# Masking local-attention scores with VectorE adds instead of TensorE matmuls, in half of the tile steps of a macaron block

## The chip, the cores and the metric

The kernel runs on one core of a Trainium2 chip. The metric is the device time of one execution in microseconds (us); three executions of the kernel before are given, and one further execution was recorded by the hardware profiler. A core has five instruction streams that matter here: TensorE (PE in the profile, with its weight loads shown apart as PEld), VectorE (DVE), ScalarE (ACT), GpSimd (POOL), and SyncE (SP), which issues all DMAs here.

## The reference

The input is x with 2048 tokens of 128 features. The block is half of a feed-forward transformer stack, a state space layer, and half of the same stack again:

```python
x = x + 0.5 * ffn_ref(layernorm(x), ...)     # 6 layers
x = x + attn_ref(layernorm(x), ...)          # state space layer (Mamba), one layer
x = x + 0.5 * ffn_ref(layernorm(x), ...)     # the same 6 layers again
```

Each of the 6 layers shifts half of the features by one token, makes queries, keys and values for 16 heads of 64, scales queries and keys to unit norm, rotates them, attends in windows of 32 tokens to the window itself and the one before, projects, adds the residual, and then does a gated feed-forward with a layer norm. What the change touches is the mask of the scores:

```python
mask = (it < jb) | (it > jb + w) | (jb == -1)
sim = jnp.einsum('bhwie,bhwje->bhwij', bq, bk2) * QK_SCALE
sim = jnp.where(mask, -jnp.finfo(sim.dtype).max, sim)
attn = jax.nn.softmax(sim, -1)
```

All arithmetic of the kernel is fp32, except that the mask is multiplied in bf16 in the kernel before.

## The kernel before

**Tiles.** The tokens are cut in tiles of 128 (four windows of 32). One pass of the stack over half of the tokens (a segment of 8 tiles) through 6 layers is 48 tiles. There are 192 tiles g = 0 to 191: first stack, segment 0 (0 to 47) and segment 1 (48 to 95), then second stack, segment 0 (96 to 143) and segment 1 (144 to 191). The state space layer of the 8 blocks of 256 tokens runs beside tiles of the middle two quarters: block s starts at step 48 + 12 s and takes some 18 steps, so it lasts from step 48 to about step 150. In the first quarter and the last one the tiles have no such work beside them.

**Steps.** The program is written out as a software pipeline. At step i each stage of the table ORDER is issued for tile g = i - lag, in the order of the table's third column (its place within the step); the stages of the state space layer are merged into the same order by their own times. [...]Feed-forward stages work on two tiles at once, so a stage of them is issued in every second step only, and steps come in two kinds:

- In every step TensorE does, in this order: the averages PX (L596), the projection of queries PQ (L372), a transpose XT (L568), the scores S (L500 masks, L511 products), the projection of keys PK (L372), the mixing ZM (L617), the transposes of queries and keys RQ and RK (L453).
- An even step adds Y (L744) ahead of PX, and F1 (L656) between S and PK. An odd step adds V (L678) ahead of PX, G (L698) between PK and ZM, and A (L698) after ZM.
- VectorE does, in every step: UK (L414, sum of squares of the keys before), SM (L546, L547, divisors), T2Q and T1Q (L398, L391, the rotation's products on the queries), MX (L528, the maxima), UQ (L414), TP (L561, the transpose of the probabilities), T1K and T2K (L391, L398, the same products on the keys), RS (L633, the residual). An odd step adds VT (L317, L318) after SM and H (L730) after RS; an even step adds YR (L758) after UK.
- ScalarE does, among others, SQ (L384, squares), ES (L522, the copy of the scores to SBUF), SK (L384), EX (L541, exponents). GpSimd does CQ and CK (L440), SB (L535, scores less maxima), AQ and AK (L408), DV (L551).

**Score stages.** S is issued at lag 2. For each parity of the heads, one bf16 matmul of a 32-row selection matrix with a 32 x 64 mask (repeated over 8 heads) starts the accumulation in a bank, and 64 small matmuls add the products. In a first tile of the sequence (`st.tok` 0) a second mask is added, which hides the window before the first. Then VectorE takes the maxima from the banks and ScalarE copies the scores to the SBUF tile `pr`. GpSimd subtracts the maxima in SBUF.

**Banks.** [...]Six form three pairs `w0`, `w1`, `w2`; `bank2` gives the pair that has been free longest, and `used` counts a pair's readers. The seventh bank is the tag "n", single: XT, F1, ZM, V and Y write into it in turn, and each must wait until the reader of the one before is done (ZM is read by RS, V by VE and VT, XT by ScalarE's L575). The last is the tag "y".

```python
    def bank(self, name, tag="n"):
        return self.ps.tile([P, 512], F32, tag=tag, name=name)
```

The tile `sq` of squares is single too (SQ, SK write it, UQ, UK read it).

Of the kernel before, what the change touches and what calls it, by code (L numbers as in the profile page):

```python
# [9 lines left out]
F32 = mybir.dt.float32  # L10
BF16 = mybir.dt.bfloat16
AF = mybir.ActivationFunctionType
ALU = mybir.AluOpType
AX = mybir.AxisListType
# [3 lines left out]
P = 128  # L18
# [3 lines left out]
HEADS = 16  # L22
DH = 64
INNER = HEADS * DH
WIN = 32
# [5 lines left out]
MASKED = -1.0e25  # L31
# [18 lines left out]
C_MASK = 256  # L50
C_MASK0 = C_MASK + 2 * WIN
C_PICK = C_MASK0 + 2 * WIN
C_PICK0 = C_PICK + P
C_RATIO = C_PICK0 + P
C_ALL = C_RATIO + 1
EXP_LN = 6
ST = 8
# [63 lines left out]
class Stream:  # L121
# [11 lines left out]
    def __init__(self, k, x, out, wp, sb, rp, ps):  # L133
        self.k, self.nc, self.x, self.out = k, k.nc, x, out
        self.wp, self.sb, self.ps = wp, sb, ps
        self.at, self.w, self.sub = [], [Ctx() for _ in range(2 * UNITS)], {}
        for g in range(TILES):
            st = Ctx()
            st.again, r = divmod(g, UNITS * ST)
            st.seg, r = divmod(r, DEPTH * ST)  # L140
            st.layer, st.t = divmod(r, ST)
            st.w = self.w[g // ST]
            st.tok = st.seg * SEG + st.t * P
            st.x, st.rot, st.sq, st.t2 = {}, {}, {}, {}
            self.at.append(st)
        self.ff = [Ctx() for _ in range(TILES // 2)]
        self.tabs = {}
        self.r0 = [rp.tile([P, SEG + 1], F32, tag=f"r0{i}", name="r0") for i in range(2)]
        self.r1 = rp.tile([P, SEG + 1], F32, tag="r1", name="r1")

        self.c0 = rp.tile([P, DEPTH], F32, tag="c0", name="c0")
        self.c1 = rp.tile([P, DEPTH], F32, tag="c1", name="c1")
        self.b1 = rp.tile([P, DEPTH, 2, 3], F32, tag="b1", name="b1")
        self.todo = {}
        self.pairs, self.pair_of, self.returned = [[0, i - 3] for i in range(3)], {}, 0
# [336 lines left out]
    def score(self, g):  # L492

        nc, k, st = self.nc, self.k, self.at[g]
        st.s = self.bank2(("s_ps", g), 2).rearrange("p j (c k) -> p j c k", k=2 * WIN)
        for par in range(2):
            rows = slice(64 * par, 64 * par + 32)
            masks = [k.mask] if st.tok else [k.mask, k.mask0]
            for lhs, rhs in masks:
                nc.tensor.matmul(  # L500
                    out=st.s[:, par],
                    lhsT=lhs[rows],
                    rhs=rhs[rows].unsqueeze(1).to_broadcast([32, 8, 2 * WIN]),
                    start=lhs is k.mask[0],
                    stop=False,
                )
        for c in range(8):
            for b in range(4):
                for par in range(2):
                    rows = slice(64 * par, 64 * par + 64)  # L510
                    nc.tensor.matmul(  # L511
                        out=st.s[32 * b : 32 * b + 32, par, c, :],
                        lhsT=st.qt[rows, c, bass.ts(b, WIN)],
                        rhs=st.kt[rows, c, bass.ds(WIN * b, 2 * WIN)],
                        start=False,
                        stop=(c == 7),
                    )

    def scores_out(self, g):
        st = self.at[g]  # L520
        st.pr = self.sb.tile([P, HEADS, 2 * WIN], F32, tag="pr", name="pr")
        self.nc.scalar.copy(st.pr.rearrange("p (c j) k -> p j c k", j=2), st.s)  # L522
        self.used("s_ps", g)

    def maxima(self, g):
        st = self.at[g]
        st.mx = self.sb.tile([P, HEADS], F32, tag="mx", name="mx")
        self.nc.vector.tensor_reduce(  # L528
            st.mx.rearrange("p (c j) -> p j c", j=2), st.s, AX.X, ALU.max
        )  # L530
        self.used("s_ps", g)

    def less(self, g):
        st = self.at[g]
# [664 lines left out]
@with_exitstack  # L1199
def macaron_kernel(  # L1200
    ctx: ExitStack,
    tc: tile.TileContext,
    x: bass.AP,
    in_w: bass.AP,
    xp_w: bass.AP,
    dt_w: bass.AP,
    out_w: bass.AP,
    wqk: bass.AP,
    wv: bass.AP,
    wo: bass.AP,  # L1210
    w1: bass.AP,
    w2: bass.AP,
    scales: bass.AP,
    vecs: bass.AP,
    cst: bass.AP,
    tabs: bass.AP,
    out: bass.AP,
):
    nc = tc.nc
    k = Ctx()  # L1220
    k.nc, k.tc = nc, tc
    k.d_in_w, k.d_xp_w, k.d_dt_w, k.d_out_w = in_w, xp_w, dt_w, out_w
    k.d_wqk, k.d_wv, k.d_wo, k.d_w1, k.d_w2, k.tabs = wqk, wv, wo, w1, w2, tabs
    k.d_sc = scales

    const = ctx.enter_context(tc.tile_pool(name="const", bufs=1))
    cs = const.tile([P, C_ALL], F32, tag="cs", name="cs")
    nc.sync.dma_start(out=cs, in_=cst)
    k.ident = cs[:, C_ID : C_ID + P]
    k.cen = cs[:, C_CEN : C_CEN + P]  # L1230
    masks = const.tile([P, 2, 2 * WIN + P], BF16, tag="masks", name="masks")
    nc.vector.tensor_copy(
        masks[:, :, 0 : 2 * WIN],
        cs[:, C_MASK : C_MASK + 4 * WIN].rearrange("p (a k) -> p a k", a=2),
    )
    nc.vector.tensor_copy(
        masks[:, :, 2 * WIN :], cs[:, C_PICK : C_PICK + 2 * P].rearrange("p (a k) -> p a k", a=2)
    )
    k.mask, k.mask0 = ((masks[:, j, 2 * WIN :], masks[:, j, 0 : 2 * WIN]) for j in range(2))
    k.ratio = cs[:, C_RATIO : C_RATIO + 1]  # L1240
    k.pv = const.tile([P, V_ALL], F32, tag="pv", name="pv")
    nc.sync.dma_start(out=k.pv, in_=vecs)
    k.ones = const.tile([P, P], F32, tag="ones", name="ones")
    nc.vector.memset(k.ones, 1.0)
    k.minus_g = const.tile([P, DEPTH], F32, tag="minus_g", name="minus_g")
    nc.vector.tensor_scalar(k.minus_g, k.pv[:, V_G : V_G + DEPTH], -1.0, None, ALU.mult)
    k.minus_nw = const.tile([P, 1], F32, tag="minus_nw", name="minus_nw")
    nc.vector.tensor_scalar(k.minus_nw, k.pv[:, V_NW : V_NW + 1], -1.0, None, ALU.mult)
    k.eps = const.tile([P, 1], F32, tag="eps", name="eps")
    nc.vector.memset(k.eps, LN_EPS)  # L1250
    k.minus_one = const.tile([P, 1], F32, tag="minus_one", name="minus_one")
    nc.vector.memset(k.minus_one, -1.0)
    k.zero = const.tile([P, 1], F32, tag="zero", name="zero")
    nc.vector.memset(k.zero, 0.0)
    xt = const.tile([P, N], F32, tag="xt", name="xt")

    dram = ctx.enter_context(tc.tile_pool(name="dram", bufs=1, space=bass.MemoryType.DRAM))

    def kept(name, shape, count):
        return [dram.tile(shape, F32, tag=f"{name}{i}", name=f"{name}{i}") for i in range(count)]  # L1260

    k.merged = kept("m", [P, 2 * INNER], DEPTH)
    k.scaled_w1 = kept("w1s", [P, 2 * FF], DEPTH)
    k.scaled_tabs = [kept(f"tab{i}_", [P, 8 * DH], 8) for i in range(DEPTH)]
    k.last_keys = kept("lk", [P, 8 * WIN], DEPTH)
    k.last_inputs = kept("li", [WIN, P], DEPTH)
    k.bc = kept("bc", [2 * NS, SUB], 8)

    with (
        tc.tile_pool(name="weights", bufs=2) as wp,  # L1270
        tc.tile_pool(name="residuals", bufs=1) as rp,
        tc.tile_pool(name="tiles", bufs=2) as sb,
        tc.tile_pool(name="banks", bufs=1, space=PSUM) as ps,
        ExitStack() as pools,
    ):
        t = Stream(k, xt, out, wp, sb, rp, ps)
        with tc.manual_schedule(engines=MANUAL):
            t.run(x, pools)


def shape_constants():


    cst = np.zeros((P, C_ALL), np.float32)
# [5 lines left out]
    cst[:, C_MASK : C_MASK + 2 * WIN] = np.where((s >= q) & (s <= q + WIN), 0.0, MASKED)  # L1290
    cst[:, C_PICK : C_PICK + P] = q == np.arange(P)[None, :] % WIN
    cst[:, C_MASK0 : C_MASK0 + 2 * WIN] = np.where((q == 0) & (s < WIN), MASKED, 0.0)
    cst[:, C_PICK0 : C_PICK0 + P] = (q == 0) & (np.arange(P)[None, :] < WIN)

    half = np.arange(0, DH, 2, dtype=np.float32)
# [12 lines left out]
    tabs = kinds.reshape(4, NB, 4, P, DH).transpose(3, 1, 0, 2, 4)  # L1308
    cst[:, C_RATIO] = np.tile(base ** (P // (WIN // 2)), 2)
    return cst, np.ascontiguousarray(tabs.astype(np.float32))  # L1310


def laid_out(i):
# [23 lines left out]
    qs, ks = i["L0_ffn_q_scale"], i["L0_ffn_k_scale"]  # L1337
    scales = np.stack([qs, swapped(qs), ks, swapped(ks)], 1).reshape(DEPTH, 4 * DH)
    cst, tabs = shape_constants()
    w = i["L0_ffn_Wqkv"]  # L1340
    return {
# [36 lines left out]
```

## Time and profile before

| | |
|---|---|
| time, median of 3 runs | 3321.47 us (3318.79 to 3322.2) |
| the profiled execution: own time, span | 3318.65 us, 3316.7 us |
| granted TensorE clock, mean | 0.996 |
| busy: PE, DVE, ACT, POOL | 97%, 85%, 77%, 88% |
| DMA queues, share of 16 engines | 18.0%, 0.7%, 0.5% |
| mask matmuls L500 | 408, 384 ns each, 77.5 us busy together |
| maxima L528 on DVE | 192, 1214 ns each |
| copies of scores L522 on ACT | 192, 1019 ns each |

The profile gives busy times of each engine, the waits that it infers from semaphores, and the chain of work that ended last. A busy time is the union of the instructions' spans; the ends of matmuls are modelled and overlap the starts of the next ones. The trace's timeline gives start, duration, engine, line, what is written and read, and the idle time just ahead with what ended it.

### The profile page before, as it was taken

The numbers are of one execution on the slowest core, as the hardware profiler recorded it, in microseconds if no ns is written. First come the engines' busy times: TensorE is split into PE (matmuls) and PEld (weight loads), VectorE is DVE, ScalarE is ACT, GpSimd is POOL, SyncE is SP. The second block draws the span as 40 slices with busy tenths as digits, with TensorE's granted clock in tenths as the row PEclk, the third lists the DMA queues.
The fourth block names the chain that finished last, engine by engine and source line by source line (L and its number), as shares of the span: only waits on it lengthen the run. The fifth ranks groups of instructions, "written<-read, shape, count | busy, mean of one in ns | idle before, by whom it ended". The sixth has DMA issues, their size and how long they took to land.

```text
span 3316.7 us, 97481 instructions
## 1 busy us (share of the span) xinstructions
PE 3207.2 (97%) x41936; PEld 2225.6 (67%) x41936; DVE 2802.8 (85%) x3540; ACT 2551.6 (77%) x4121; POOL 2907.3 (88%) x2317
## 2 busy tenths in 40 slices
PE   7999999999999999999999999999999999999997
PEld 4677677676666666666666666666666676777765
DVE  5778888887898989889989889898988888888884
ACT  6777777778778778787787877877777777777775
POOL 6999999998988989889888898898988888988983
PEclk9999999999999999999999999999999999999999
DMA  8222221221211122121211122111121111111000
GB/s 259 76 67 65 66 67 58 71 68 45 59 52 43 47 53 56 50 61 37 56 51 54 47 53 57 42 52 53 52 63 39 31 41 44 32 36 43 20 11 9
DMA packets 134494, 181.26 MB, mean 55 GB/s; under 512 B 13176, under 2 KB 91312, under 8 KB 127152
## 3 DMA queue, kind: packets, MB, share of 16 engines
q1 hardware_dynamic: 134064, 175.04, 18.0%
q8 instruction: 330, 5.41, 0.7%
q14 instruction: 100, 0.82, 0.1%
HBM read 138.75 MB, written 24.05 MB: 49 GB/s over the span
## 4 chain that ended last, share of the span: by engine, by line
PE 69%; DVE 12%; ACT 9%; POOL 7%; issue 2%; DMA 0%; SPq 0%; POOLq 0%; DVEq 0%; ACTq 0%
PE x_ps L372 16%; PE y_ps L617 16%; PE z_ps L596 8%; PE t_ps L453 8%; PE s_ps L511 6%; PE g_ps L698 3%; PE o_ps L744 3%; PE a_ps L698 3%; DVE da L1055 2%; DVE rot L391 2%; POOL rot L440 2%; DVE t L398 2%; PE y_ps L1089 2%; ACT da L1044 1%; ACT sq L384 1%
## 5 line engine op out<-in xcount | busy, mean ns | idle before, releaser
L408 POOL TENSOR_TENSOR rot<-rot,t 128x1024 f32<-128x1024 f32 x384 | 900.7, 2368 | 10.6 <-DVE rot L391 6.1
L372 PE MATMUL x_ps<-qk,r 128*128 128x512 f32 x1536 | 753.4, 613 | 29.6 <-ACT zt L608 10.1
L617 PEld LDWEIGHTS y_ps<-zt,m 128*128 128x128 f32 x6144 | 715.1, 192 | 63.8 <-ACT xc L667 36.6
L440 POOL TENSOR_TENSOR rot<-rot,rn 128x1024 f32<-128x1024 f32 x384 | 722.4, 1902 | 14.4
L617 PE MATMUL y_ps<-zt,m 128*128 128x128 f32 x6144 | 718.6, 275 | 5.3 <-ACT xc L667 3.1
L384 ACT ACTIVATE sq<-x_ps 128x1024 f32<-128x1024 f32 x384 | 393.2, 1024 | 276.3 <-DVE rot L391 229.9
L398 DVE TENSOR_TENSOR t<-x_ps,tab 128x1024 f32<-128x1024 f32 x384 | 467.7, 1218 | 154.6 <-PE i_ps L568 84.4
L551 POOL TENSOR_TENSOR pr<-pr,rs 128x1024 f32<-128x1024 f32 x192 | 365.2, 1902 | 198.8 <-DVE rs L547 174.0
L372 PEld LDWEIGHTS x_ps<-qk,r 128*128 128x128 f32 x1536 | 271.7, 190 | 361.8 <-issue 232.8
L391 DVE TENSOR_TENSOR rot<-x_ps,tab 128x1024 f32<-128x1024 f32 x384 | 467.3, 1217 | 20.0 <-ACT sq L384 19.5
L608 ACT COPY zt<-z_ps 128x1024 f32<-128x1024 f32 x384 | 368.9, 1010 | 140.8 <-PE z_ps L596 140.6
L414 DVE TENSOR_REDUCE ss<-sq 128x16 f32<-128x1024 f32 x384 | 466.5, 1215 | 7.7 <-ACT sq L384 5.0
L596 PE MATMUL z_ps<-pt,xw 32*128 32x512 f32 x3072 | 402.5, 614 | 3.1 <-DVE t L398 1.4
L535 POOL TENSOR_TENSOR pr<-pr,mx 128x1024 f32<-128x1024 f32 x192 | 365.3, 1903 | 25.9 <-ACT carry L1066 19.4
L453 PE MATMUL t_ps<-cs,rot 128*128 128x128 f32 x3072 | 370.9, 273 | 4.3 <-DVE sc L1076 2.1
L453 PEld LDWEIGHTS t_ps<-cs,rot 128*128 128x128 f32 x3072 | 344.1, 141 | 32.7 <-issue 9.8
L511 PE MATMUL s_ps<-kt,qt 64*32 64x64 f32 x24576 | 287.3, 225 | 0.5 <-issue 0.5
L511 PEld LDWEIGHTS s_ps<-kt,qt 64*32 64x32 f32 x24576 | 255.9, 105 | 47.1 <-issue 46.0
L541 ACT ACTIVATE pr<-pr 128x1024 f32<-128x1024 f32 x192 | 203.2, 1058 | 106.9 <-POOL pr L535 106.1
L596 PEld LDWEIGHTS z_ps<-pt,xw 32*128 32x128 f32 x3072 | 146.6, 184 | 163.4 <-issue 129.6
L561 DVE STREAM_TRANSPOSE pt<-pr 128x1024 f32<-128x1024 f32 x192 | 237.0, 1234 | 2.3 <-POOL pr L551 2.3
L546 DVE TENSOR_REDUCE rs<-pr 128x16 f32<-128x1024 f32 x192 | 232.9, 1213 | 6.2 <-ACT pr L541 3.3
(144 smaller groups left out, 4809.0 us busy)
## 6 DMA issues: line engine op xcount, KB each, us to landing
bc<-bc SPq DMA_DIRECT2D x64, 512.0 KB, 5.4
tab<-tab SPq DMA_DIRECT2D x120, 256.0 KB, 2.6
qk<-in_wqk_dram SPq DMA_DIRECT2D x24, 1024.0 KB, 5.0
m<-m SPq DMA_DIRECT2D x24, 1024.0 KB, 5.3
tab<-in_tabs_dram SPq DMA_DIRECT2D x48, 256.0 KB, 2.9
xw<-xw SPq DMA_DIRECT2D x192, 48.0 KB, 3.3
m<-mst SPq DMA_DIRECT2D x6, 1024.0 KB
w<-w1s SPq DMA_DIRECT2D x18, 341.0 KB, 3.5
```

Of the source, the lines that this page charges most:

```text
L372: nc.tensor.matmul(out=x[:, j], lhsT=self.columns(g), rhs=st.w.qk[:, bass.ds(kind * INNER + j * 512, 512)], start=True, stop=True,)
L384: self.nc.scalar.activation(st.sq[kind], st.x[kind], AF.Square)
L391: self.nc.vector.tensor_tensor(st.rot[kind], st.x[kind], cos, ALU.mult)
L398: self.nc.vector.tensor_tensor(st.t2[kind].rearrange("p h (two c) -> p h two c", two=2), st.x[kind].rearrange("p h (two c) -> p h two c", ...
L408: self.nc.gpsimd.tensor_tensor(st.rot[kind], st.rot[kind], st.t2[kind], ALU.add)
L414: self.nc.vector.tensor_reduce(st.ss[:, kind, :], st.sq[kind], AX.X, ALU.add)
L440: self.nc.gpsimd.tensor_tensor(st.rot[kind], st.rot[kind], st.rn[:, kind, :].unsqueeze(2).to_broadcast([P, HEADS, DH]), ALU.mult,)
L453: self.nc.tensor.transpose(t_ps[:, c, :], flat[:, bass.ts(c, P)], self.k.ident)
L511: nc.tensor.matmul(out=st.s[32 * b : 32 * b + 32, par, c, :], lhsT=st.qt[rows, c, bass.ts(b, WIN)], rhs=st.kt[rows, c, bass.ds(WIN * b, 2 ...
L596: self.nc.tensor.matmul(out=st.z[b // 2][:, b % 2].rearrange("p (h q) -> p h q", q=WIN), lhsT=st.xw[rows, j, :], rhs=st.pt[rows, :, j, :], ...
L608: self.nc.scalar.copy(st.zt[:, 2 * half : 2 * half + 2].rearrange("p b h q -> p b (h q)"), st.z[half])
L617: self.nc.tensor.matmul(out=st.y_ps.rearrange("p (b q) -> p b q", q=WIN), lhsT=st.w.m[:, h // 2, h % 2, :], rhs=st.zt[:, :, h, :], start=( ...
```

## The change

A tile is `quiet` when its stack number equals its segment number: tiles 0 to 47 and 144 to 191, 96 of 192. For a quiet tile

- S issues no mask matmuls; each product matmul starts and stops its own 32 x 64 output;
- ES does nothing: no ScalarE copy;
- MX makes the tile `pr`, adds the mask to the scores in two VectorE instructions (one for each bank, 128 x 512, PSUM and a repeated 128 x 64 fp32 mask in SBUF, to SBUF), and takes the maxima from `pr` in SBUF. Both counts of the pair are given back there.

The constants get 64 more columns for the mask of a first tile (C_FIRST), 32 KB more in the load of `cst` at the start. For other tiles the code is as before. ORDER, and with it the place of MX, is the same.

```diff
+            st.quiet = st.again == st.seg
...
     def score(self, g):
...
-        for par in range(2):
-            rows = slice(64 * par, 64 * par + 32)
-            masks = [k.mask] if st.tok else [k.mask, k.mask0]
-            for lhs, rhs in masks:
-                nc.tensor.matmul(
...
+        if not st.quiet:
+            for par in range(2):
...
-                        start=False,
-                        stop=(c == 7),
+                        start=st.quiet,
+                        stop=st.quiet or c == 7,
                     )
 
     def scores_out(self, g):
         st = self.at[g]
+        if st.quiet:
+            return
...
     def maxima(self, g):
-        st = self.at[g]
+
+        nc, k, st = self.nc, self.k, self.at[g]
         st.mx = self.sb.tile([P, HEADS], F32, tag="mx", name="mx")
-        self.nc.vector.tensor_reduce(
-            st.mx.rearrange("p (c j) -> p j c", j=2), st.s, AX.X, ALU.max
-        )
-        self.used("s_ps", g)
+        if st.quiet:
+            st.pr = self.sb.tile([P, HEADS, 2 * WIN], F32, tag="pr", name="pr")
+            mask = k.added if st.tok else k.added0
+            mask = mask.unsqueeze(1).to_broadcast([P, 8, 2 * WIN])
+            pr = st.pr.rearrange("p (c j) k -> p j c k", j=2)
+            for par in range(2):
+                nc.vector.tensor_tensor(pr[:, par], st.s[:, par], mask, ALU.add)
+            self.used("s_ps", g)
+            self.used("s_ps", g)
+            nc.vector.tensor_reduce(st.mx, st.pr, AX.X, ALU.max)
+        else:
+            nc.vector.tensor_reduce(
+                st.mx.rearrange("p (c j) -> p j c", j=2), st.s, AX.X, ALU.max
+            )
+            self.used("s_ps", g)
```

More of the change, by code (lines that the diff above doesn't have):

```diff
@@ L53 @@
 C_PICK0 = C_PICK + P
-C_RATIO = C_PICK0 + P
+C_FIRST = C_PICK0 + P
+C_RATIO = C_FIRST + 2 * WIN
 C_ALL = C_RATIO + 1
@@ L495, in score @@
         st.s = self.bank2(("s_ps", g), 2).rearrange("p j (c k) -> p j c k", k=2 * WIN)
-        for par in range(2):
-            rows = slice(64 * par, 64 * par + 32)
-            masks = [k.mask] if st.tok else [k.mask, k.mask0]
-            for lhs, rhs in masks:
[L500 to L505, printed above, removed]
-                )
+        if not st.quiet:
+            for par in range(2):
+                rows = slice(64 * par, 64 * par + 32)
+                masks = [k.mask] if st.tok else [k.mask, k.mask0]
+                for lhs, rhs in masks:
+                    nc.tensor.matmul(
+                        out=st.s[:, par],
+                        lhsT=lhs[rows],
+                        rhs=rhs[rows].unsqueeze(1).to_broadcast([32, 8, 2 * WIN]),
+                        start=lhs is k.mask[0],
+                        stop=False,
+                    )
         for c in range(8):
@@ L525, in maxima @@
     def maxima(self, g):
-        st = self.at[g]
+        nc, k, st = self.nc, self.k, self.at[g]
         st.mx = self.sb.tile([P, HEADS], F32, tag="mx", name="mx")
-        self.nc.vector.tensor_reduce(
-            st.mx.rearrange("p (c j) -> p j c", j=2), st.s, AX.X, ALU.max
-        )
-        self.used("s_ps", g)
+        if st.quiet:
[11 more added lines that the diff above has]
+                st.mx.rearrange("p (c j) -> p j c", j=2), st.s, AX.X, ALU.max
+            )
+            self.used("s_ps", g)
     def less(self, g):
@@ L1239, in macaron_kernel @@
     k.mask, k.mask0 = ((masks[:, j, 2 * WIN :], masks[:, j, 0 : 2 * WIN]) for j in range(2))
+    k.added = cs[:, C_MASK : C_MASK + 2 * WIN]
+    k.added0 = cs[:, C_FIRST : C_FIRST + 2 * WIN]
     k.ratio = cs[:, C_RATIO : C_RATIO + 1]
@@ L1292, in shape_constants @@
     cst[:, C_MASK0 : C_MASK0 + 2 * WIN] = np.where((q == 0) & (s < WIN), MASKED, 0.0)
+    cst[:, C_FIRST : C_FIRST + 2 * WIN] = cst[:, C_MASK : C_MASK + 2 * WIN]
+    cst[0:WIN, C_FIRST : C_FIRST + WIN] = MASKED
     cst[:, C_PICK0 : C_PICK0 + P] = (q == 0) & (np.arange(P)[None, :] < WIN)
```

## The prediction

> **What bounds the kernel now.** I read the busy shares first, then a window for each quiet stretch (the tiles without state space work beside them), then the chain of waits there, then the timeline of one pair of steps, since an even and an odd step together repeat.
>
> ```profile
> PE 3207.2 (97%) x41936; PEld 2225.6 (67%) x41936; DVE 2802.8 (85%) x3540; ACT 2551.6 (77%) x4121; POOL 2907.3 (88%) x2317
> PE 69%; DVE 12%; ACT 9%; POOL 7%; issue 2%; DMA 0%; SPq 0%; POOLq 0%; DVEq 0%; ACTq 0%
> 120.00:780.00 660.00, 652.79 (x9018) 461.82 (x9019) 541.02 (x677) 504.11 (x781) 617.22 (x486) 1.00 0.20 66
> 2610.00:3230.00 620.00, 620.00 (x8604) 441.02 (x8606) 519.07 (x635) 475.30 (x728) 544.33 (x423) 1.00 0.11 33
> ```
>
> The last two lines are the quiet stretches; after the length come busy PE, PEld, DVE, ACT, POOL. PE has no gap (652.79 of 660, 620.00 of 620), DVE is at 82% and 84%. The chain in the second stretch is PE alone, piece after piece:
>
> ```profile
> 2912.07 0.32 PE s_ps L500 x2
> 2912.39 1.41 PE s_ps L511 x91
> ...
> 2919.72 1.75 PE t_ps L453 x16
> 2921.47 0.43 PE v_ps L678 x2
> 2921.90 1.93 PE z_ps L596 x16
> ```
>
> So each pair of mask matmuls is 0.32 us of the engine that sets the pace. But a saturated engine also says that the others arrive just in time or earlier; how much earlier is what the change spends. VectorE in the same even step (start, duration, line; idle time ahead in brackets):
>
> ```profile
> 2912.05 1.23 DVE L398 TENSOR_TENSOR t<-x_ps,tab 128x1024 f32<-128x1024 f32 x1 [1.38 <-PE x_ps L372]
> 2913.19 1.21 DVE L391 TENSOR_TENSOR rot<-x_ps,tab 128x1024 f32<-128x1024 f32 x1
> 2914.33 1.21 DVE L528 TENSOR_REDUCE mx<-s_ps 128x16 f32<-128x1024 f32 x1
> ...
> 2919.01 1.21 DVE L398 TENSOR_TENSOR t<-x_ps,tab 128x1024 f32<-128x1024 f32 x1
> 2920.14 0.58 DVE L633 TENSOR_TENSOR r<-y_ps,r 64x128 f32<-64x128 f32 x2
> 2921.20 0.30 PEld L678 LDWEIGHTS v_ps<-sq,ones 128*128 128x128 f32 x2
> ```
>
> It is released by the end of PQ, and from T2Q at 2912.05 to the end of RS at 2920.72 (2920.14 + 0.58) it has no idle time at all. RS reads the mixing result out of the single bank "n". V, the next writer of that bank on PE, loads at 2921.20, only 0.48 after. That V waits for RS is seen where RS came late, at the start of the kernel:
>
> ```profile
> 119.33 0.57 DVE L633 TENSOR_TENSOR r<-y_ps,r 64x128 f32<-64x128 f32 x2
> 120.02 0.30 PEld L678 LDWEIGHTS v_ps<-sq,ones 128*128 128x128 f32 x2 [0.40 <-issue]
> 120.05 0.67 PE L678 MATMUL v_ps<-sq,ones 128*128 128x256 f32 x2 [0.19 <-DVE r L633]
> ```
>
> Here the load follows RS's end (119.90) by 0.12, PE having been idle. So V's slack is 0.48 - 0.12 = 0.36 us.
>
> [...]1217 ns for 1024 from PSUM (L391), 424 ns for 256 (L993), which gives 688 for 512 on a straight line.[...]ACT's squares of the queries start at 2914.44, after T1Q's end at 2914.40 on the same banks.
>
> **The change, part by part**, for a quiet tile.
>
> *Removed from PE*: two mask matmuls, 0.32 us on the chain (four for a first tile, one tile in each of 6 layers). At most 96 x 0.32 + 6 x 0.32 = 33 us.
>
> *Removed from ACT*: one copy L522, 1.02 us. ACT is 77% busy, and the squares around it wait for VectorE, so I give nothing for it. The subtraction on POOL loses this source and waits for the maxima alone.
>
> *Added on DVE*: two adds of 128x512. A following instruction starts about 0.08 before the end of the one ahead (L391 at 2917.86 lasts 1.23, L398 starts at 2919.01), so the first add takes 0.69 - 0.08 = 0.61; the second feeds the maxima and is taken whole, 0.69, with 0.03 ahead of a dependent instruction (L546 ends at 2923.10, L547 starts at 2923.13). The maxima keep their 1.21: L414 reads SBUF at 1215 ns, L528 PSUM at 1214. Sum 1.33 us. The operation in this form is not in the trace: below it is bounded by 2 x 0.61 = 1.22, above by 2 x 0.69 + 0.06 = 1.44. No reason for a gain here.
>
> *Behind it on DVE, even step*: UQ, TP, T1K, T2K, RS, then UK, SM. None of them waited before, so RS is 1.33 later, against a slack of 0.36: V comes 0.97 later. [...]PX, PQ, XT behind V are 0.97 later as well, though their own data is there. The 0.32 saved earlier in this step is lost in front of V. Nothing is later next: T2K's banks, which PX takes over, are free before RS; XT needs VT, and RS to VT (UK, SM, L547, VT: 3.5 us) is shorter than V to XT (4.4).
>
> *Odd step*: T2Q starts when PQ ends, as before. PE would be 0.32 ahead after S, but G takes over the queries' pair, which ScalarE squares only after T1Q:
>
> ```profile
> 2928.24 1.02 ACT L384 ACTIVATE sq<-x_ps 128x1024 f32<-128x1024 f32 x1 [1.40 <-DVE rot L391]
> 2929.38 1.12 PEld L698 LDWEIGHTS g_ps<-q,w 128*128 128x128 f32 x6 [0.70 <-issue]
> ```
>
> G loads 0.12 after the squares' end at 2929.26, so it cannot come forward by more than about 0.1. Then T2K is 1.33 later; RQ loads 1.40 after T2K's end at 2934.03 and takes over its pair, a slack of 1.40 - 0.12 = 1.28: about 0.05 late. After T2K, VectorE has waits of 0.53 (RS), 0.79 (H), 0.58 (YR) and 1.38 (T2Q), 3.28 in all, which take up the rest. Odd steps: nothing, between -0.1 and +0.2.
>
> *POOL and the queues*: L535 starts at 2917.49 behind CK, the maxima end at 2915.54 + 1.33: still covered by 0.6. No DMA moves[...].
>
> *Sum*. The gap from RS to V repeats over a layer's four even steps: 0.46, 0.46, 0.78, 0.24 in the first stretch, 0.47, 0.47, 0.47, 0.18 in the second (means 0.48 and 0.40; slacks 0.36 and 0.28). Even steps with V behind them: 22 in the first, some 22 in the second that are not covered by the last state space block. 22 x (1.33 - 0.36) + 22 x (1.33 - 0.28) = 21 + 23 = 44 us. The first steps, before there is a V, and the tail may give back 2. So +42: the profiled execution's own 3318.65 would be 3361; the median of the runs lies 2.8 above it, so **3363 us**.
>
> **Rivals.** *Faster*: V is not held, the mask matmuls' time is gained. This would need RS's place on DVE not to depend on MX, or an add that overlaps other work. For it speaks the saturated PE and DVE at only 84%; against it the unbroken DVE row above. Price: -33 us would be 3289; but with G held by the squares (and ZM in even steps by XC, loading at 2915.78 right after XC behind those squares) about 0.25 a pair of steps, 47 pairs, -12: 3310. It wins only if the delay at RS is under 0.36, so an addition of under a third of 1.33. Chance 0.12. *No change*: the delay is about 0.5, or the two effects cancel; 3321, chance 0.04. *My forecast*: chance 0.68, with additions of 1.22 to 1.44 (44 even steps x 0.11 = 5 us either way) and odd steps of -0.1 to +0.2 (-4 to +9): 3350 to 3378. *Slower still*: VectorE also stops the odd steps at RQ, or POOL's second addition L408, which in even steps starts at 2921.7 while T2K would end at 2921.55, becomes late: 0.3 to 0.5 a pair more, +14 to +23, 3377 to 3386. Chance 0.16. That the adds are not issued as said has no sign in the diff.
>
> **The numbers.** About 0.2% (6.6 us) is what can be told from no change here. Slower 0.68 + 0.16 = 0.84, faster 0.12, same 0.04. The slower cases' own range is 3338 to 3390; to hold 8 in 10 the range begins at 3325 and ends at 3392.
>
> **What would show it.** Right: in quiet even steps DVE runs unbroken from T2Q to RS, 1.33 us longer; ahead of V a repeating PE gap of about 1.3 us named after L633; the pair of steps takes about 31.7 instead of 30.74; middle stretch as before; DVE's two adds at about 0.69 each. Wrong: pairs of 30.5 or less, no gap at V; or adds of under 0.5 us.

## The result and the profile after

The changed kernel takes 3367.25 us (median of 4 runs, 3366.33 to 3370.48) against 3320.18 us before in the same runs: a ratio of 1.0143, interval 1.0125 to 1.0161. It is slower by 47 us. The profiled execution took 3370.48 us (span 3368.3). In the changed file the residual RS is L650, the variances V are L695, T2Q and T2K L400, T1Q and T1K L393, the adds L540.

The page's busy shares, the engines' shares of the chain, and two windows of the quiet stretches (length; busy PE, PEld, DVE, ACT, POOL; clock):

```profile
PE 3207.9 (95%) x41732; PEld 2216.4 (66%) x41732; DVE 2917.3 (87%) x3732; ACT 2465.4 (73%) x4025; POOL 2913.6 (86%) x2317
PE 53%; DVE 26%; ACT 10%; POOL 7%; issue 3%; DMA 0%; SPq 0%; DVEq 0%; POOLq 0%; ACTq 0%
120.00:780.00 660.00, 633.94 (x8706) 444.71 (x8705) 573.86 (x740) 451.77 (x716) 604.47 (x475) 0.99 0.20 63
2640.00:3280.00 640.00, 617.38 (x8519) 435.33 (x8521) 567.07 (x716) 439.80 (x691) 545.67 (x422) 1.00 0.10 32
```

PE was busy for all of 620 us in the second stretch before; now 22.6 of 640 us are idle, though PE has less to do. VectorE's share of the chain has more than doubled, yet at 567 of 640 us VectorE is not full. The waits by engine name the place:

```profile
PE v_ps L695 <- DVE r L650: 34.4, 42, 1.1
PE g_ps L715 <- ACT sq L386: 13.1, 42, 0.8
```

Each line gives the sum, the number of waits and the longest one. Before, the first pair stood with 0.7 us in 2 waits and the second, the wait of G in odd steps, with 3.6 us in 5. The timeline of one even step and the start of the next one, VectorE first, then PE's loads and matmuls:

```profile
2982.52 1.23 DVE L400 TENSOR_TENSOR t<-x_ps,tab 128x1024 f32<-128x1024 f32 x1 [1.38 <-PE x_ps L374]
2983.67 1.22 DVE L393 TENSOR_TENSOR rot<-x_ps,tab 128x1024 f32<-128x1024 f32 x1
2984.80 1.28 DVE L540 TENSOR_TENSOR pr<-s_ps,cs 128x512 f32<-128x512 f32 x2
2986.11 1.22 DVE L543 TENSOR_REDUCE mx<-pr 128x16 f32<-128x1024 f32 x1
...
2990.75 1.22 DVE L400 TENSOR_TENSOR t<-x_ps,tab 128x1024 f32<-128x1024 f32 x1
2991.99 0.15 DVE L646 COPY r<-c 64x1 f32<-64x1 f32 x1
2992.16 0.59 DVE L650 TENSOR_TENSOR r<-y_ps,r 64x128 f32<-64x128 f32 x2
```

```profile
2989.82 1.78 PEld L455 LDWEIGHTS t_ps<-cs,rot 128*128 128x128 f32 x16
2992.87 0.30 PEld L695 LDWEIGHTS v_ps<-sq,ones 128*128 128x128 f32 x2 [1.27 <-ACT qt L464]
2992.90 0.67 PE L695 MATMUL v_ps<-sq,ones 128*128 128x256 f32 x2 [1.06 <-DVE r L650]
```

The maxima start 1.31 us after the first add does (2984.80 to 2986.11), so that is what the adds put in front of everything behind them. VectorE then runs without a gap to RS, which ends at 2992.75 (2992.16 + 0.59), and V's load follows 0.12 later, after 1.27 us of idle weight loading. (This is one of the every-fourth even steps that has the small copy L646 in front of RS.) The load row names ACT, the matmul row DVE: of two releasers named for one wait, the one that had just ended is RS (L464 ended at 2992.01). What stands behind V in PE's program came later with it: the averages PX had their probabilities (L578 ended at 2989.60) and their banks (T2K ended at 2991.97), but their first matmul is at 2993.50, 0.60 after V's, where it was 0.53 after V's before (2921.30 to 2921.83).

How much later RS is shows in an ordinary even step of the changed kernel, from T2Q to the end of RS:

```profile
2760.47 1.22 DVE L400 TENSOR_TENSOR t<-x_ps,tab 128x1024 f32<-128x1024 f32 x1 [1.60 <-PE x_ps L374]
2769.82 0.58 DVE L650 TENSOR_TENSOR r<-y_ps,r 64x128 f32<-64x128 f32 x2
```

That is 9.93 us (2769.82 + 0.58 - 2760.47), against 8.67 before (2912.05 to 2920.72). So of the 1.31 us, 1.26 arrive at RS. Part of the rest is a short wait that the timeline doesn't mark: before, UQ started 1.17 after the maxima (2914.33 to 2915.50), and now it starts 1.14 after them (2986.11 to 2987.25).

From XT of an even step to XT of the next, the timeline gives 13.78 us before (2911.80 to 2925.58), and now 14.70, or 14.98 in steps like this one. The odd step takes 16.96 in both.

### The profile page after: what moved, and what is told of

Read it like the earlier page. It is cut to its first block, busy times and chain, and to the rows that moved or that the text cites. A ratio compares the mean times of both kernels' runs of the same rounds, so it can differ in the third digit from the quotient of the medians.

```text
span 3368.3 us, 97252 instructions
## 1 busy us (share of the span) xinstructions
PE 3207.9 (95%) x41732; PEld 2216.4 (66%) x41732; DVE 2917.3 (87%) x3732; ACT 2465.4 (73%) x4025; POOL 2913.6 (86%) x2317
## 4 chain that ended last, share of the span: by engine, by line
PE 53%; DVE 26%; ACT 10%; POOL 7%; issue 3%; DMA 0%; SPq 0%; DVEq 0%; POOLq 0%; ACTq 0%
PE x_ps L374 12%; PE y_ps L634 11%; PE z_ps L613 8%; DVE rot L393 6%; DVE t L400 6%; PE t_ps L455 5%; PE g_ps L715 3%; PE o_ps L761 3%; PE a_ps L715 3%; DVE ss L416 3%; PE s_ps L514 2%; ACT sq L386 2%; DVE da L1072 2%; POOL rot L442 2%; DVE pt L578 2%
## 5 line engine op out<-in xcount | busy, mean ns | idle before, releaser
L410 POOL TENSOR_TENSOR rot<-rot,t 128x1024 f32<-128x1024 f32 x384 | 901.7, 2370 | 12.3 <-DVE rot L393 6.4
L400 DVE TENSOR_TENSOR t<-x_ps,tab 128x1024 f32<-128x1024 f32 x384 | 467.9, 1219 | 187.8 <-PE i_ps L585 113.1
L393 DVE TENSOR_TENSOR rot<-x_ps,tab 128x1024 f32<-128x1024 f32 x384 | 467.6, 1218 | 13.4 <-ACT sq L386 12.8
L578 DVE STREAM_TRANSPOSE pt<-pr 128x1024 f32<-128x1024 f32 x192 | 237.2, 1235 | 2.1 <-POOL pr L568 2.1
```

The costliest lines, as they stand in the source:

```text
L393: self.nc.vector.tensor_tensor(st.rot[kind], st.x[kind], cos, ALU.mult)
L400: self.nc.vector.tensor_tensor(st.t2[kind].rearrange("p h (two c) -> p h two c", two=2), st.x[kind].rearrange("p h (two c) -> p h two c", ...
L410: self.nc.gpsimd.tensor_tensor(st.rot[kind], st.rot[kind], st.t2[kind], ALU.add)
```

## The experiments

The theory: V waits for RS because the bank "n" is single, RS stands behind the adds in VectorE's order, and PX, PQ and XT stand behind V in PE's. Its rival: work added to VectorE counts wherever it stands. All times are medians, ratios are against the kernel before in the same runs.

**odd_tiles and even_tiles.** The change for one parity of the quiet tiles.

```diff
-            st.quiet = st.again == st.seg
+            st.quiet = st.again == st.seg and g % 2 == 1
```

> The adds only for quiet tiles with an odd number, so MX with adds falls in odd steps (lag 2), where V is not behind RS; even quiet tiles as before. Theory (V in the step after an even step is held by RS over the bank n): odd steps cost nothing, 3320 us, between 3313 and 3325. Rival (the 1.24 us of VectorE work counts wherever it stands, half of the tiles give half of the loss): 3343 us.

Measured: 3322.8 us, 1.0007 (0.9999 to 1.0016).

> The adds only for quiet tiles with an even number, odd quiet tiles as before. Theory: the whole loss is here, 3365 us, between 3360 and 3370, with the step from an even XT to the odd one at 14.7 us and the other at 16.96. Rival (VectorE work counts wherever it stands): 3343 us.

Measured: 3365.73 us, 1.0134 (1.0119 to 1.0149). Half of the adds carry the whole loss, the other half none. In odd_tiles VectorE's row of an ordinary odd step (XT at 2776.68), with PE's load for RQ, shows where the added time goes:

```profile
2779.22 1.28 DVE L540 TENSOR_TENSOR pr<-s_ps,cs 128x512 f32<-128x512 f32 x2
...
2785.17 1.22 DVE L400 TENSOR_TENSOR t<-x_ps,tab 128x1024 f32<-128x1024 f32 x1
2786.30 0.58 DVE L650 TENSOR_TENSOR r<-y_ps,r 64x128 f32<-64x128 f32 x2
2786.53 1.89 PEld L455 LDWEIGHTS t_ps<-cs,rot 128*128 128x128 f32 x16
2787.03 1.26 DVE L747 SCALAR_TENSOR_TENSOR h<-a_ps,b,gl 128x256 f32<-128x256 f32 x3
...
2789.99 0.98 DVE L775 SCALAR_TENSOR_TENSOR r<-o_ps,pv,r 64x256 f32<-64x256 f32 x2 [0.58 <-PE o_ps L761]
```

Before, L633 (here L650) and L730 (L747) of an odd step each stood behind an idle time, 0.53 and 0.79 us. The first is gone, and 0.15 is left of the second (2786.30 + 0.58 to 2787.03); the next wait, for Y's result, is 0.58 as before: the added work has taken the place of waiting. RQ, whose banks T2K must have left, loads 9.85 us after XT in both kernels, but now only 0.14 after T2K's end (2786.39), where it was 1.40: the delay only just fits here.

**v_in_y and before_v_in_y.** The wait taken away, VectorE's work left as it is: V of quiet tiles writes to bank "y".

```diff
-        ff.v_ps = self.bank("v_ps")[:, 0:SUB]
+        ff.v_ps = self.bank("v_ps", "y" if self.first(f).quiet else "n")[:, 0:SUB]
```

> As the changed kernel, but the variances V of quiet pairs of tiles are written to the bank y, which is nearly unused there, in place of the bank n, so V does not wait for RS any more; VectorE's work is the same. Theory: PX's next gate, T2K's pair, has 1.48 us of slack against 1.24, so PE sets the pace again: 3310 us, between 3300 and 3325, and no gap ahead of V. Rival (VectorE's longer work itself, or a gate right behind V, is the bound): 3350 to 3367 us.

Measured: 3321.09 us, 1.0000 (0.9991 to 1.0008). The whole loss is gone with all adds in place: even steps are back at 13.69, and V's wait for RS is no longer in the list of PE's waits. The time is at the upper end of what was expected, because PE gains less than thought (see no_masks) and the start of the kernel and the end of the state space stretch give some of it back (see the last experiments).

> The kernel before with the variances V of quiet pairs in the bank y, nothing else. Theory: V did not wait for RS there, so nothing changes: 3321 us, between 3316 and 3325. Rival (the other bank is worth time by itself, and what it gave beside the adds was not the wait on RS alone): 3280 us, as much less as it took off the changed kernel.

Measured: 3323.49 us, 1.0009 (1.0000 to 1.0017). By itself the other bank is worth nothing.

**dose128 and dose512.** One unneeded add on VectorE ahead of the maxima, in even quiet tiles of the kernel before (n stands for 2 or 8 heads; two lines that define `quiet` and `added` as in the changed kernel are left out).

```diff
+        if st.quiet and g % 2 == 0:
+            extra = self.sb.tile([P, n, 2 * WIN], F32, tag="extra", name="extra", bufs=1)
+            mask = self.k.added.unsqueeze(1).to_broadcast([P, n, 2 * WIN])
+            self.nc.vector.tensor_tensor(extra, st.s[:, 0, 0:n], mask, ALU.add)
```

> The kernel before with one unneeded VectorE add of 128x128 (0.21 us net) ahead of the maxima in even quiet tiles. Theory: the slack between RS and V of 0.34 (0.06 to 0.12 in every fourth even step) takes it: 1 to 2 us, 3322 us. Rival (what is added to VectorE counts in full): 46 x 0.21 = 10 us, 3331 us.

Measured: 3322.89 us, 1.0006 (0.9997 to 1.0015). In the second stretch three even steps of four are unchanged at 13.78 us, the fourth takes 13.86.

> As dose128 with one add of 128x512 (0.60 us net). Theory: 0.60 less the slack of each even step (0.34, 0.34, 0.66, 0.12 in the first stretch, 0.35, 0.35, 0.35, 0.06 in the second): 22 x 0.25 + 22 x 0.32 = 13 us, 3334 us. Rival: 46 x 0.60 = 28 us, 3349 us.

Measured: 3330.1 us, 1.0029 (1.0018 to 1.0039): 9.5 us more, nearer to the theory's 13 than to 28. In the second stretch even steps take 13.97, 0.19 longer, and the fourth 14.26, 0.48 longer. An ordinary even step of dose512, VectorE first, then the load of V:

```profile
2733.29 1.23 DVE L399 TENSOR_TENSOR t<-x_ps,tab 128x1024 f32<-128x1024 f32 x1 [1.60 <-PE x_ps L373]
2741.93 0.58 DVE L638 TENSOR_TENSOR r<-y_ps,r 64x128 f32<-64x128 f32 x2
2742.62 0.30 PEld L683 LDWEIGHTS v_ps<-sq,ones 128*128 128x128 f32 x2 [0.16 <-issue]
```

From T2Q to the end of RS it takes 9.22 us, so RS is 0.55 later than before (8.67), and V again follows it by about 0.12. A delay of 0.55 that costs 0.19 leaves a slack of 0.36; the change itself, 1.26 that cost 0.92 (14.70 - 13.78), gives 0.34. In the fourth step it is 0.07 (0.55 - 0.48) and 0.06 (1.26 - 1.20). So the cost here was a delay less a slack, in dose512 (0.55) and in the change itself (1.26), and not a share of a busy engine.

**adds_and_masks.** The adds come on top of the mask matmuls.

```diff
-        if not st.quiet:
+        if True:
...
-                        start=st.quiet,
-                        stop=st.quiet or c == 7,
+                        start=False,
+                        stop=(c == 7),
```

> As the changed kernel, but quiet tiles keep their mask matmuls too (the mask is then added twice), so that PE saves nothing. Theory: what PE saves is lost in front of V and of G, so keeping the masks costs nothing: 3367 us, between 3362 and 3373. Rival (PE still sets the pace and the saving is inside the measured sum): 0.32 x 102 = 33 us more, 3400 us.

Measured: 3362.12 us, 1.0121 (1.0104 to 1.0138). Keeping the masks does not cost 33 us; it costs nothing. In quiet steps the two kernels agree (14.70 and 16.96). That this one is even 5 us under the changed kernel comes from elsewhere and is taken up under the hardware.

**no_masks.** PE's part alone.

```diff
         if st.quiet:
-            return
...
-            for par in range(2):
-                nc.vector.tensor_tensor(pr[:, par], st.s[:, par], mask, ALU.add)
```

> The part of the change on PE alone: quiet tiles issue no mask matmuls, and get no adds either; ScalarE's copy and the maxima stay as before. It leaves out the mask of the quiet tiles. Theory: G in odd steps and ZM in even steps are held by ScalarE's squares, so PE gains at most 0.10 to 0.25 us a pair of steps: 3314 us, between 3307 and 3320. Rival (PE sets the pace in every step): 33 us, 3288 us.

Measured: 3315.23 us, 0.9984 (0.9977 to 0.9991): 5 us. Even steps take 13.69, odd ones 16.96 as before, so of 0.64 us of masks in a pair of steps 0.09 is gained. ScalarE and PE's load for ZM in an even step show the gate, the wait that takes the gain away:

```profile
2913.84 1.02 ACT L386 ACTIVATE sq<-x_ps 128x1024 f32<-128x1024 f32 x1 [1.63 <-DVE rot L393]
2914.76 0.37 ACT L671 COPY xc<-c_ps 128x256 f32<-128x256 f32 x1
2915.17 3.65 PEld L621 LDWEIGHTS y_ps<-zt,m 128*128 128x128 f32 x32 [0.78 <-ACT xc L671]
```

ZM writes to the bank "n" as well, so it waits until ScalarE's XC has emptied it, and XC stands behind the squares. Before, the same wait was 0.46 and hidden under the matmuls ahead. ZM loads 3.98 us after XT here (2911.19 to 2915.17) as before (2911.80 to 2915.78), so the 0.32 saved ahead of it is lost at this place; the 0.09 come behind it (ZM's load to V's takes 5.32 where it took 5.42). This kernel keeps ScalarE's copy of the scores and v_in_y does not, and both take 13.69, so taking the copy away gains nothing here.

**v_in_y_xc, before_xc and v_in_y_xc_quiet.** To take that gate away, F1 and XC are moved ahead of SQ, in all steps and then in quiet ones alone.

```diff
-    ... ("F1", 5, 0.634), ... ("XC", 5, 0.669), ...
+    ... ("F1", 5, 0.596), ... ("XC", 5, 0.597), ...
```

> As the changed kernel with V in the bank y, and F1 and XC moved ahead of SQ in the step (0.596 and 0.597 in place of 0.634 and 0.669), in all steps, so that ScalarE empties bank n for ZM before it does the squares. Theory: of the 0.32 us that the masks took, even steps got back 0.10 and now get the other 0.22, 46 x 0.22 = 10 us: 3311 us, between 3304 and 3317. Rival (another gate right behind: RQ, or the squares now late for UQ): 3318 to 3326 us.

Measured: 3349.37 us, 1.0084 (1.0069 to 1.0099). Both were wrong on the total. Quiet even steps did fall, to 13.55, by 0.14 where the theory had 0.22, but steps beside state space work became longer.

> The kernel before with F1 and XC moved in the same way, as a control. Theory: the squares of the queries end some 0.4 us later, UQ with them, just under V's slack: 3322 us, between 3318 and 3328, no gain. Rival (the order is better by itself): 3311 us or less.

Measured: 3350.58 us, 1.0091 (1.0074 to 1.0107). It was expected at 3322. One line of ScalarE's waits in before_xc:

```profile
ACT xc L667 <- PE c_ps L656: 176.0, 86, 7.6
```

In the kernel before this is 24.5 us in 19 waits. Of the 176.0 us, 89.7 in 39 waits lie in the middle stretch, between 850 and 2500 us. The squares, which stand behind XC, came later there: VectorE's UQ and UK (L414) wait for them for 25.9 us in 37 waits, against 5.0 us in the whole kernel before. The expectation rested on quiet steps only.

> As v_in_y_xc, but F1 and XC are moved ahead of SQ only in steps without state space work (below 48 and above 150); the other steps keep their order. Theory: the loss of some 30 us lay in the middle stretch alone, where ScalarE then waits for F1, and the even steps of the quiet stretches keep their 13.55 us: 3313 us, between 3307 and 3319. Rival (the loss comes with the order in the quiet steps too): 3340 us or more.

Measured: 3320.52 us, 1.0001 (0.9992 to 1.0009), outside the expected range. The 30 us are gone, so they lay in the middle stretch; but the gain of some 9 us in the regular quiet steps is given back: 5.2 us between the first step and XT of tile 10, 2.8 between tiles 144 and 146. At both places PE's granted clock (third number from the end) is lower:

```profile
60.00:100.00 40.00, 35.16 (x486) 24.82 (x486) 30.03 (x38) 27.49 (x43) 35.23 (x35) 0.91 0.44 138
2540.00:2580.00 40.00, 37.45 (x459) 26.73 (x458) 36.37 (x48) 23.23 (x37) 29.06 (x24) 0.96 0.12 38
```

In the window from 120 to 140 us it is 0.83. The kernel before has 0.96, 1.00 and 1.00 in these three windows. As an estimate, the clock takes 8.6 us here (40 x 0.09 + 40 x 0.04 + 20 x 0.17) and 1.6 before, a difference of 7.0 of the 8.0 given back. Of this kernel's 13 executions the three with a mean clock of 0.995 took 3314.11, 3316.28 and 3318.73 us, the others, at 0.992 to 0.994, 3319.85 or more.

**v_in_y_xc_inner.** The tiles at the ends are left as in the kernel before (the edit is against v_in_y_xc_quiet).

```diff
-            st.quiet = st.again == st.seg
+            st.quiet = 8 <= g < 46 or g >= 150
...
-            early = {"F1": 0.596, "XC": 0.597} if i < 48 or i > 150 else {}
+            early = {"F1": 0.596, "XC": 0.597} if 10 <= i < 48 or i > 152 else {}
```

> As v_in_y_xc_quiet, but the first 8 tiles and those at the two ends of the state space stretch (46, 47 and 144 to 149) are treated as in the kernel before. Theory: the gain of the regular quiet steps (in v_in_y_xc_quiet 4.9 us from tile 8 to 46 and 3.2 us from tile 148 to 190) is kept, and the 5 us lost by tile 8 and the 3 us lost between tiles 144 and 148 go: 3312 us, between 3307 and 3316. Rival (the loss at the ends is variation of the granted clock, not of these tiles): 3318 to 3322 us.

Measured: 3314.76 us, 0.9984 (0.9978 to 0.9991), about 5 us under the kernel before and 52 under the changed one. By tile 10 it is 0.2 us behind the kernel before, and between tiles 144 and 146 it loses nothing; the clock is 1.00 in all three windows, and 0.995 or 0.996 in the mean of each of its 21 executions. So the lower clock goes with the treatment of these tiles, where the rival had it vary by itself; how the one brings the other is not shown. This version beats both, by little over the kernel before: VectorE's adds were worth having here where their delay met waiting, with a bank for V and an early XC.

## Why the prediction was right

*What bounds*: the reading that PE sets the pace and that VectorE has 0.36 us to spare at one place held. Read from dose512, the slack at V is 0.36, and 0.07 in the fourth step, where the forecast had 0.06 for the second stretch. (That PE has no gap holds for the second stretch; in the first, 7 of 660 us were idle.)

*The adds*: priced at 0.69 each and 1.33 together. They are 0.68 each and put 1.31 in front of the maxima:

```profile
L540 DVE TENSOR_TENSOR pr<-s_ps,cs x192: 675/681/692, 46.8 to 3314.7; 128x512 f32<-128x512 f32 x192
```

*Even steps*: forecast 0.97 longer in the first stretch and 1.05 in the second. Measured 0.91, and 1.20 in the fourth, which is a mean of 0.98 in the second. The first stretch has a mean of 0.89, two steps of four with 0.91, one with 0.60 (14.10 to 14.70) and one with 1.14. The term that was too large, by 0.07, is the delay at RS, 1.26 where the forecast had 1.33: 0.02 of it lies in the adds, and VectorE's row was not quite without waiting.

*Odd steps*: forecast nothing; 16.96 in both. even_tiles and odd_tiles show it whole. But RQ had a slack of 1.28 against a delay of 1.26, so there was hardly any room. Only the step into a new layer of the first stretch falls, from 19.02 to 18.69.

*PE's saving*: forecast lost, which adds_and_masks shows for the sum. The place was wrong for even steps: the forecast has the 0.32 lost in front of V, with a PE gap of about 1.3 there, and the gap is 0.82 in the mean (34.4 us in 42 waits), because the 0.32 is lost at ZM, a gate that the forecast names only under its rivals. In odd steps it is lost at G, as forecast: the 42 waits for the squares take 0.31 in the mean. The rival's price of 0.25 a pair of steps without V's wait was too high: no_masks and v_in_y give 0.09.

*The sum*: +44 from the two stretches, -2 from the ends. In the profiled executions the time from XT of tile 8 to that of tile 46 grows by 15.4 us and from tile 148 to 190 by 21.5. These are 37 of the 51.7 us between the two spans, from 40 of the 44 even steps. (The medians differ by 47; the profiled execution was the slowest of the four.) The term for the ends had the wrong sign: 3.9 us are lost, not gained, by tile 8. And "middle stretch as before" missed 7.3 us between tiles 48 and 144. The granted clock, 0.994 against 0.996 over the spans, is worth some 7 of the 51.7 us, as an estimate (3368.3 x 0.006 - 3316.7 x 0.004); the forecast had no term for it. The mechanism was right, but the near agreement of 3363 with 3367 is in part luck: even steps cost a little less than forecast, and other terms cost more.

*The rivals*: the faster one needed the delay at RS to be under its slack; it was 1.26 against 0.36. The slower one, RQ and L408 becoming late, is not seen: odd steps are unchanged, and in the even step from 2982.52 POOL's two additions (L410 in the changed file) run from 2989.83 for 4.69 us without a wait, where they took 4.71 before.

## What to carry to other kernels

Here PE was saturated, and moving work off it paid only as far as its next gate: 0.09 of 0.64 us in a pair of steps. Work put on VectorE, which has idle time, cost nothing where that idle time lay behind the insertion and ahead of the next instruction that PE waits for (odd_tiles, 1.0007), and the whole loss where it did not (even_tiles, 1.0134). So take the row of the receiving engine from the insertion to each hand-over, count the idle time in it, and add the slack at the hand-over: here 0.36 against 1.26 in one kind of step; in the other 1.28 at one hand-over and 1.32 of idle time ahead of the next, just enough. The delay crossed over at a single buffer, the bank "n", and with another bank for V the loss was gone (3321.09 us against 3367.25). So give such a writer another bank first, and try moves of order in every kind of step, not only in the quiet ones (before_xc, 1.0091).

## What the runs showed of the hardware

The granted clock of TensorE is not the same in all these kernels: its mean over the profiled executions is 0.993 to 0.997. Windows of the start, changed kernel first and adds_and_masks second (the third number from the end is the clock):

```profile
120.00:140.00 20.00, 18.93 (x204) 11.43 (x203) 13.23 (x19) 13.26 (x23) 17.17 (x15) 0.83 0.17 60
```

```profile
120.00:140.00 20.00, 19.21 (x227) 13.24 (x226) 16.56 (x23) 16.77 (x28) 19.16 (x17) 1.00 0.25 83
```

As an estimate, a clock of 0.83 over 20 us takes 3.4 us of PE time (20 x 0.17), about the 3.9 that the changed kernel is behind at tile 8; adds_and_masks is 0.3 behind there. The windows of 1000 to 1100, 1600 to 1700, 1900 to 2000 and 2300 to 2400 us show 0.98 in the changed kernel, as an estimate 2 us each (100 x 0.02), where the kernel before has 0.98 in the first of them alone; over the whole span 0.994 was granted, against 0.996 before. The same dip near 124 to 128 us is in the five other kernels whose even tiles give up their masks from the start of the kernel (even_tiles, no_masks, v_in_y, v_in_y_xc, v_in_y_xc_quiet), in none of the rest. In that place of the changed kernel PE waits twice, for V and inside PX:

```profile
120.87 0.67 PE L695 MATMUL v_ps<-sq,ones 128*128 128x256 f32 x2 [0.50 <-DVE r L650]
...
123.17 3.47 PE L613 MATMUL z_ps<-pt,xw 32*128 32x512 f32 x12 [0.58 <-ACT qt L464]
```

The 12 matmuls of the last row take 3.47 us; at the same place of the kernel before they take 1.99 (L596, at 122.36). The wait inside PX was there before too, without a dip, and in before_xc PE waits longer here in sum, 1.22 for V and 0.28 inside PX, also without one. So waiting alone does not tell the kernels apart. The dip goes with masks left out of the first even tiles, in these six kernels of fourteen. What brings it is not shown, as no run held the clock apart from the rest, and why the dips in the middle stretch, where the program is the same, are more in the changed kernel stays open.
